# A local-attention stage on one Trainium2 core: its period in a new order, with the scores in two halves

## The chip, the core and the metric

The program runs on one core of a Trainium2 chip. Its engines work side by side, each through its own queue of instructions in order: TensorE (PE; its weight loads are shown apart, as PEld), VectorE (DVE), ScalarE (ACT), GpSimd (POOL), and SyncE (SP), which here issues DMAs. They wait for each other by semaphores. The products go to PSUM, which this kernel divides into eight banks, each a tile of 128 x 512 fp32; VectorE and ScalarE read them there.

The metric is the device time of one execution in microseconds (us): the median of three runs. The trace comes from one more execution, under the profiler.

## What is computed

The reference is a chain of eight blocks on `x` of shape (4, 512, 128): cross-attentions, two mixtures of experts, a ternary feed-forward. The change touches the sixth, `_L2_ffn`: a local transformer of six layers with 16 heads of 64, windows of 32 tokens that look one window back, keys and queries of unit length with rotary factors, a token shift, and a gated feed-forward of 341 hidden units.

```python
def attn_layer(x, Wqkv, qs, ksc, Wo):
    q, k, v = jnp.split(x @ Wqkv, 3, -1)
    ...
    q = l2norm(q) * qs
    k = l2norm(k) * ksc
    q = q * cos * scale + rotate_half(q) * sin * scale
    k = k * cos * inv + rotate_half(k) * sin * inv
    out = local_attention(q, k, v)
    return out.transpose(0, 2, 1, 3).reshape(b, n, INNER) @ Wo

def local_attention(q, k, v):
    ...
    bk2, bv2 = (look(bk), look(bv))     # this window and the one before it
    sim = jnp.einsum('bhwie,bhwje->bhwij', bq, bk2) * QK_SCALE
    sim = jnp.where(mask, -jnp.finfo(sim.dtype).max, sim)
    attn = jax.nn.softmax(sim, -1)
    return jnp.einsum('bhwij,bhwje->bhwie', attn, bv2).reshape(b, h, n, d)
```

Around it, per layer: `x + attn_layer(shift_tokens(x))`, then the feed-forward with a layer norm, a GELU gate and the two products.

## The kernel before

All of this stage is in `local_transformer` (from L1804). The rows live transposed in `Y[b]`, 128 features x 512 tokens, one for each of the four rows of the batch. A **tile** is 128 tokens of one row in one layer: 6 x 4 x 4 = 96 tiles, in the order of layers, rows, tokens. One **period** of the loop over `n` starts tile `n` and carries on the two before it: `T` is tile `n`, `T1` the one before, `T2` the one before that. A row's feed-forward, `F`, is spread over four periods ("phases"), once all of its tiles have their attention. The order of instructions is written out by hand (`tc.manual_schedule()`): each engine runs its instructions in the order in which the loop issues them, so that order is what the change rewrites. In a period stand, with their engines:

- `queries_or_keys(T, kind, c)` (L1835): one product of 512 columns into a PSUM bank (L1842), and its Square on ScalarE (L1844). Four to a tile: kind 0 queries, 1 keys; c the half of the heads.
- `rotate(T, kind, c)` (L1847): three operations on VectorE, the two rotary products from PSUM (L1852, L1855) and the sum of squares (L1864), then GpSimd's addition (L1865).
- `normalise(T)` (L1868): inverse lengths of all queries and keys, small operations of GpSimd (L1875 to L1881) around ScalarE's Ln and Exp (L1876, L1877), then four scalings on GpSimd (L1884), queries first.
- `turned(T1, kind)` (L1886): eight transposes on TensorE by the helper `to_features` (L617, recorded as L621) and two copies on ScalarE (L1896). For keys GpSimd puts the last window of the tile before in front (L1892, or zeros, L1894).
- `scores(T1)` (L1932): eight small products that write the mask (L1940), then 64 products of 64x32 weights with 64 columns, recorded as 128 (L1949), all into two banks.
- `softmax(T1)` (L1955): on VectorE the largest (L1959) and the subtraction (L1960), on ScalarE Exp (L1965).
- `probabilities(T2)` (L1967): eight transposes of P, two copies on ScalarE (L1970).
- `average(T2, g)` (L1972): 32 small products, recorded as 64, for half of the heads (L1980); `normalised(T2, g)` (L1987) divides on VectorE (L1989, L1990). Both halves use the same two banks in turn.
- `attended(T2)` (L1995): eight transposes of the averages, two copies on ScalarE. `project_out(T2)` (L2001): 16 products of 128 columns (L2004) into the averages' banks; `residual(T2)` (L2007) adds them to `Y` on VectorE (L2011).
- `values(T, x0)` (L1905): a product of 512 columns (L1919), ScalarE's copy (L1920), and DMAs on SP's queue (L1922 to L1930) that shift values by a window; they are read two periods later.
- the feed-forward in `ff_stage` (L2074): in phase 0 transposes and moments, later `ff_norm`, four scalings on VectorE (L559); in phase 1 transposes back and two gate products; in phase 2 the third gate product and two up products; in phase 3 the third and the down product. They use the scores' banks.

PSUM: two banks for the products, two for transposes and values (`p_tr`), two for scores and feed-forward (`pair("sc")`), two for averages and projection (`pair("av")`). A piece that takes a bank waits until its last reader is done.

On TensorE a period runs: queries 0, P's transposes, queries 1, the feed-forward's first piece, average 0, queries turned, keys product 0, average 1, keys turned, keys product 1, averages' transposes, all scores, projection, both values, the feed-forward's second piece.

Of the kernel before, what the change touches and what calls it, by code (L numbers as in the profile page):

```python
# [21 lines left out]
F32 = mybir.dt.float32  # L22
# [4 lines left out]
ALU = mybir.AluOpType  # L27
# [3 lines left out]
NT = S // 128  # L31
# [241 lines left out]
def tile_kernel(ctx: ExitStack, tc: tile.TileContext, A: dict, out: bass.AP):  # L273
# [1530 lines left out]
    def local_transformer(Y, lf, lw, columns, tabs):  # L1804

        with ExitStack() as es:
# [21 lines left out]
            class Tile:  # L1828


                def __init__(self, i, b, tt):
                    self.i, self.b, self.tt = i, b, tt
                    self.rot, self.raw, self.ss = {}, {}, None

# [32 lines left out]

            def normalise(T):  # L1868


                n = 2 * LH
                ss = T.ss.rearrange("p a b -> p (a b)")
                y = small.tile([128, n], F32, name="rn_y")
                t = small.tile([128, n], F32, name="rn_t")
                G.tensor_scalar(ss, ss, 1e-24, -0.5, ALU.max, ALU.mult)  # L1875
                SC.activation(y, ss, AF.Ln, scale=-2.0)  # L1876
                SC.activation(y, y, AF.Exp, scale=-0.5)  # L1877
                G.tensor_tensor(t, y, y, ALU.mult)
                G.tensor_tensor(t, t, ss, ALU.mult)
                G.tensor_scalar(t, t, 1.5, None, ALU.add)  # L1880
                G.tensor_tensor(y, y, t, ALU.mult)  # L1881
                for (kind, c), a in sorted(T.rot.items()):
                    o = LH * kind + 8 * c
                    G.tensor_tensor(a, a, bc(y[:, o : o + 8], [128, 8, LD], 2), ALU.mult)  # L1884

            def turned(T, kind):  # L1886


                lead = 32 * kind
                t = qp.tile([128, LH // 2, lead + 128], F32, name="kT" if kind else "qT")  # L1890
                if kind and T.tt:
                    G.tensor_copy(t[:, :, 0:32], T.before.kT[:, :, 128:160])  # L1892
                elif kind:
                    G.memset(t[:, :, 0:32], 0.0)  # L1894
                for c in range(2):
# [3 lines left out]
                    )  # L1899
                if kind:  # L1900
                    T.kT = t
                else:
                    T.qT = t

# [26 lines left out]

            def scores(T):  # L1932

                T.banks = pair("sc").rearrange("p z (k d) -> p z k d", d=64)
                for w in range(4):
                    for z in range(2):
                        r = slice(64 * (z ^ (w // 2)), 64 * (z ^ (w // 2)) + 64)
                        PE.matmul(  # L1940
                            T.banks[32 * w : 32 * w + 32, z], identb[r, r.start : r.start + 32],
                            maskw[r, int(w + T.tt == 0)], start=True, stop=False,
                            skip_group_check=True,
                        )
                for k in range(LH // 2):
                    for w in range(4):
# [7 lines left out]

            def softmax(T):  # L1955

                P = tp.tile([128, LH // 2, 2, LD], F32, name="P", bufs=1)
                mx = small.tile([128, 2, LH // 2], F32, name="la_mx")
                V.tensor_reduce(mx, T.banks, AX.X, ALU.max)  # L1959
                V.tensor_tensor(  # L1960
                    P.rearrange("p k z d -> p z k d"), T.banks,
                    bc(mx, [128, 2, LH // 2, LD], 3), ALU.subtract,
                )
                T.P = P.rearrange("p k z d -> p k (z d)")
                SC.activation(T.P, T.P, AF.Exp, scale=8.0)  # L1965
# [55 lines left out]

            def ff_norm(F):
                layernorm(F.xn, F.xn, F.found)

# [48 lines left out]

            def ff_stage(F, phase, second):  # L2074
                F.w1, F.w2 = loaded[F.i][2:]
                if phase == 0 and not second:
                    ff_moments(F)
                elif phase == 1:
                    ff_gate(F, 0, 1) if second else ff_turn(F)
                elif phase == 2 and second:  # L2080
                    ff_up(F, 0, 1)
                elif phase == 2:
                    ff_gate(F, 2)
                    SC.preload_act_table_set(EXP_LN)
                elif phase == 3:
                    ff_down(F) if second else ff_up(F, 2)

            tiles = [Tile(i, b, tt) for i in range(DEPTH) for b in range(B) for tt in range(NT)]  # L2090
# [3 lines left out]
            SC.preload_act_table_set(EXP_LN)  # L2094
            for n in range(len(tiles) + 2):
                T = tiles[n] if n < len(tiles) else None
                T1 = tiles[n - 1] if 0 <= n - 1 < len(tiles) else None
                T2 = tiles[n - 2] if 0 <= n - 2 < len(tiles) else None
                m, phase = divmod(n - 6, 4)
                F = rows[m] if 0 <= m < len(rows) else None  # L2100
                if T:
# [12 lines left out]
                    T.tabs = tabs[T.i]  # L2114
                    queries_or_keys(T, 0, 0)
                if T2:
                    probabilities(T2)
                if T:
                    queries_or_keys(T, 0, 1)
                    rotate(T, 0, 0)  # L2120
                if F:
                    ff_stage(F, phase, False)
                if T2:
                    average(T2, 0)
                if T1:
                    turned(T1, 0)
                if T:
                    queries_or_keys(T, 1, 0)
                if T2:
                    normalised(T2, 0)  # L2130
                if T:
                    rotate(T, 0, 1)
                if T2:
                    average(T2, 1)
                if T1:
                    turned(T1, 1)
                if T:
                    queries_or_keys(T, 1, 1)
                if T2:
                    normalised(T2, 1)  # L2140
                if T:
                    rotate(T, 1, 0)
                if T2:
                    attended(T2)
                if T and T.tt == NT - 1 and n + 1 < len(tiles):
                    swap(tiles[n + 1].b)
                if T1:
                    scores(T1)
                if T:
                    rotate(T, 1, 1)  # L2150
                if T:
                    normalise(T)
                if T1:
                    softmax(T1)
                if T2:
                    project_out(T2)
                    residual(T2)
                if F and phase == 0:
                    ff_norm(F)
                if T:  # L2160
                    values(T, 0)
                    values(T, 1)
                if F:
                    ff_stage(F, phase, True)
            return loaded[DEPTH - 1][2:]
# [133 lines left out]
```

## Time and profile before

| | us |
|---|---|
| median of three runs (2460.44 to 2462.8) | 2462.42 |
| the profiled execution, its own time | 2456.04 |
| its span, first to last instruction | 2454.2 |
| first query product of the local stage starts | 516.4 |
| first query product of its last tile starts | 2125.35 |
| mean distance of such products, tiles 10 to 90 | 17.01 |
| mean granted clock of TensorE over the span | 0.953 |

The 96 tiles of the local stage take two thirds of the span. In the profile's rows, "PE" with a line number is a matmul group of TensorE, "x2" or "x128" the instructions merged in it; each fp32 product is recorded as two matmuls with a weight load each. In brackets stands the idle time of the engine just before, and what ended it; "issue" means that nothing which the profile shows ended it. A line with a window in front gives busy us and instruction counts of PE, PEld, DVE, ACT and POOL in that window, then granted clock, DMA share and GB/s. Queue q8 is one of the two that carry instructions.

### The profile page before, as it was taken

Reading aid. Unit: us, or ns where it says so; the run is one execution under the profiler, and the core shown is the slowest. Engines: PE = TensorE matmul, PEld = TensorE weight load, DVE = VectorE, ACT = ScalarE, POOL = GpSimd, SP = SyncE. Lnnn points to the kernel's source line nnn. Section 1 sums busy time; section 2 is a strip of 40 time slices with the busy share of each in tenths; the row PEclk is TensorE's granted clock in tenths of the full one; section 3 lists DMA queues with packets and bytes.
Section 4 is the critical chain, followed back from the end, with each engine's and each line's share of the span. In section 5 each row is a group of like instructions: output and inputs, shape, how many; then the busy total and the mean of one; then the engine's idle time right before and its main releaser. Section 6 shows DMA issues by size and latency. Waiting matters only on the chain. (4 is left out here: it accounts for less than half of the span.)

```text
span 2454.2 us, 86703 instructions
## 1 busy us (share of the span) xinstructions
PE 2228.0 (91%) x37341; PEld 1479.5 (60%) x37341; DVE 1759.3 (72%) x3896; ACT 1298.1 (53%) x2389; POOL 1338.6 (55%) x1862
## 2 busy tenths in 40 slices
PE   7958969978999999999999999999999999989676
PEld 3536734546666666666666666666666666644355
DVE  5545356866888888777887888887878788767422
ACT  3423325645666655666666666565666666525222
POOL 2141330256667676766667766766667666710433
PEclk9868989988999999999999999999999999989688
DMA  7201110016211121111211121111211111120023
GB/s 182 68 21 41 40 60 2 1 41 135 80 35 29 35 70 36 33 29 35 75 31 36 29 79 33 29 35 27 80 31 31 35 29 35 27 67 23 26 67 95
DMA packets 134298, 116.14 MB, mean 47 GB/s; under 512 B 29506, under 2 KB 102701, under 8 KB 133917
## 3 DMA queue, kind: packets, MB, share of 16 engines
q1 hardware_dynamic: 122037, 99.67, 15.8%
q0 software_dynamic: 4608, 7.35, 0.9%
q8 instruction: 296, 4.85, 0.9%
q10 hardware_dynamic: 7271, 3.58, 0.5%
q14 instruction: 86, 0.70, 0.1%
HBM read 42.84 MB, written 21.52 MB: 26 GB/s over the span
## 5 line engine op out<-in xcount | busy, mean ns | idle before, releaser
L1865 POOL TENSOR_TENSOR rc<-rc,rs 128x512 f32<-128x512 f32 x384 | 489.8, 1276 | 400.7 <-DVE rs L1855 326.3
L1842 PE MATMUL ps_mm<-wqk,y 128*128 128x512 f32 x768 | 397.2, 599 | 5.3 <-issue 3.5
L1884 POOL TENSOR_TENSOR rc<-rc,rn_y 128x512 f32<-128x512 f32 x384 | 388.6, 1044 | 7.5
L1852 DVE TENSOR_TENSOR rc<-ps_mm,tabs 128x512 f32<-128x512 f32 x384 | 262.5, 684 | 129.8 <-ACT sq L1844 126.5
L1844 ACT ACTIVATE sq<-ps_mm 128x512 f32<-128x512 f32 x384 | 231.2, 602 | 161.4 <-PE ps_mm L1842 108.0
L1855 DVE TENSOR_TENSOR rs<-ps_mm,tabs 128x512 f32<-128x512 f32 x384 | 261.5, 681 | 0.2 <-POOL rc L1865 0.2
L1864 DVE TENSOR_REDUCE ss<-sq 128x8 f32<-128x512 f32 x384 | 259.5, 676 | 0.0
L621 PE MATMUL ps_tr<-cst,rc 128*128 128x128 f32 x1536 | 210.9, 280 | 4.3 <-POOL rc L1884 4.0
L1980 PEld LDWEIGHTS ps_av<-v,PT 64*32 64x32 f32 x12288 | 138.1, 105 | 126.5 <-PE ps_tr L621 54.1
L2004 PE MATMUL ps_av<-aT,wo 128*128 128x128 f32 x1536 | 200.7, 283 | 2.4 <-issue 2.4
L2004 PEld LDWEIGHTS ps_av<-aT,wo 128*128 128x128 f32 x1536 | 181.0, 193 | 12.6 <-issue 3.9
L621 PEld LDWEIGHTS ps_tr<-cst,rc 128*128 128x128 f32 x1536 | 165.6, 142 | 24.4 <-POOL rc L1884 5.1
L1949 PE MATMUL ps_sc<-kT,qT 64*32 64x64 f32 x12288 | 148.1, 225 | 33.6 <-issue 32.9
L1980 PE MATMUL ps_av<-v,PT 64*32 64x65 f32 x12288 | 170.3, 225 | 6.2 <-DVE attn L1990 1.7
L1949 PEld LDWEIGHTS ps_sc<-kT,qT 64*32 64x32 f32 x12288 | 141.2, 105 | 44.2 <-issue 38.1
L1056 POOL DMA_INDIRECT back<-ye,to x80 | 78.8, 985 | 147.5 <-DVE ye L1170 104.0
L1842 PEld LDWEIGHTS ps_mm<-wqk,y 128*128 128x128 f32 x768 | 124.5, 192 | 56.3 <-issue 50.1
L1965 ACT ACTIVATE P<-P 128x1024 f32<-128x1024 f32 x96 | 101.4, 1057 | 97.3 <-DVE P L1960 97.3
L1876 ACT ACTIVATE rn_y<-ss 128x32 f32<-128x32 f32 x96 | 22.0, 229 | 237.9 <-POOL ss L1875 237.9
L802 ACT ACTIVATE P<-ps,deltaT 77x512 f32<-77x512 f32 x192 | 115.8, 683 | 56.7 <-PE ps L796 53.0
L1896 ACT COPY qT<-ps_tr 128x512 f32<-128x512 f32 x192 | 103.3, 589 | 74.6 <-PE ps_tr L621 74.3
L1959 DVE TENSOR_REDUCE la_mx<-ps_sc 128x16 f32<-128x1024 f32 x96 | 116.9, 1218 | 31.0 <-PE ps_sc L1949 31.0
(399 smaller groups left out, 4368.9 us busy)
## 6 DMA issues: line engine op xcount, KB each, us to landing
v<-v SPq DMA_DIRECT2D x432, 65.0 KB
v<-v SPq DMA_DIRECT2D x96, 195.0 KB
wqk<-in_L_ffn_Wqkv_dram SPq DMA_DIRECT2D x24, 256.0 KB
sent<-xn SPq DMA_DIRECT2D x2, 2210.0 KB
xe<-sent SPq DMA_DIRECT2D x16, 260.0 KB
back<-xn SPq DMA_DIRECT2D x2, 2048.0 KB
raw<-in_L_ffn_W_dram SPq DMA_DIRECT2D x8, 512.0 KB
w<-in_L_ffn_W_dram SPq DMA_DIRECT2D x16, 256.0 KB
```

Source lines behind the costliest of these rows:

```text
L621: PE.transpose(t[:, i], src[:, i], ident)
L1842: PE.matmul(t, lhs, T.w[2 * kind + c], start=True, stop=True)
L1844: SC.activation(sq, t, AF.Square)
L1852: V.tensor_tensor(a, t, bc(T.tabs[:, 2 * kind, tt], [128, 8, LD], 1), ALU.mult)
L1855: V.tensor_tensor(r.rearrange("p h (x d) -> p h x d", x=2), t.rearrange("p h (x d) -> p h x d", x=2)[:, :, ::-1], bc(T.tabs[:, 2 * kind + ...
L1864: V.tensor_reduce(T.ss[:, kind, 8 * c : 8 * c + 8], sq, AX.X, ALU.add)
L1865: G.tensor_tensor(a, a, r, ALU.add)
L1884: G.tensor_tensor(a, a, bc(y[:, o : o + 8], [128, 8, LD], 2), ALU.mult)
L1949: PE.matmul(T.banks[32 * w : 32 * w + 32, z, k], T.qT[r, k, 32 * w : 32 * w + 32], T.kT[r, k, 32 * w : 32 * w + 64], start=False, stop=Tru ...
L1959: V.tensor_reduce(mx, T.banks, AX.X, ALU.max)
L1980: PE.matmul(T.means[32 * w : 32 * w + 32, x0, k], T.PT[r, 4 * g + k, 32 * w : 32 * w + 32], (T.v1 if w % 2 else T.v2)[r, x0, 4 * g + k], s ...
L2004: PE.matmul(t, T.wo[:, c], T.aT[:, c], start=(c == 0), stop=(c == 7))
```

## The change

The period becomes a table of stages, each with its lag in tiles, and the loop walks through it. Some functions are cut in two so that the table can place their parts: `normalise` into `inverse_norms` and `normalise(T, kind)`, `softmax` into `largest` and `exponentials`, `scores` into two halves of four of its eight column groups, the keys' first window of `turned` into `keys_before`, `ff_stage` into `ff_first` and `ff_second`. The computation stays the same, and so do all buffers.

On TensorE a period now runs: values 0, keys product 0, P's transposes, the feed-forward's second piece (one period later than before), average 0, queries product 1, keys turned, the feed-forward's first piece, queries turned, average 1, keys product 1, mask and scores' first half, queries product 0, averages' transposes, scores' second half, values 1, projection. `residual` stands at the head of the next period, `ff_norm` behind it. VectorE's rotation of queries product 0 stands in front of `largest`. The loop has one period more.

```diff
+            def inverse_norms(T):
...
+                T.inv = y
+
+            def normalise(T, kind):
+                for c in range(2):
+                    a, o = T.rot[kind, c], LH * kind + 8 * c
+                    G.tensor_tensor(a, a, bc(T.inv[:, o : o + 8], [128, 8, LD], 2), ALU.mult)
...
+            def keys_before(T):
+
+                T.kT = qp.tile([128, LH // 2, 160], F32, name="kT")
+                if T.tt:
+                    G.tensor_copy(T.kT[:, :, 0:32], T.before.kT[:, :, 128:160])
                 else:
+                    G.memset(T.kT[:, :, 0:32], 0.0)
...
-            def scores(T):
...
+            def scores(T, g):
+                if g == 0:
+                    T.banks = pair("sc").rearrange("p z (k d) -> p z k d", d=64)
...
-                for k in range(LH // 2):
+                for k in range(4 * g, 4 * g + 4):
...
+            def largest(T):
+                T.mx = small.tile([128, 2, LH // 2], F32, name="la_mx")
+                V.tensor_reduce(T.mx, T.banks, AX.X, ALU.max)
+
+            def exponentials(T):
                 P = tp.tile([128, LH // 2, 2, LD], F32, name="P", bufs=1)
...
+            period = (
+                (values, 0, 0),
+                (residual, 3),
+                (ff_norm, 1),
+                (queries_or_keys, 0, 1, 0),
+                (rotate, 0, 1, 0),
+                (keys_before, 1),
+                (probabilities, 2),
+                (ff_second, 1),
+                (average, 2, 0),
+                (queries_or_keys, 0, 0, 1),
+                (turned, 1, 1),
+                (normalised, 2, 0),
+                (rotate, 0, 0, 1),
+                (ff_first, 0),
+                (turned, 1, 0),
+                (average, 2, 1),
+                (queries_or_keys, 0, 1, 1),
+                (normalised, 2, 1),
+                (scores, 1, 0),
+                (queries_or_keys, 0, 0, 0),
+                (attended, 2),
+                (rotate, 0, 1, 1),
+                (scores, 1, 1),
+                (rotate, 0, 0, 0),
+                (values, 0, 1),
+                (largest, 1),
+                (inverse_norms, 0),
+                (normalise, 0, 0),
+                (project_out, 2),
+                (normalise, 0, 1),
+                (exponentials, 1),
+            )
...
-            for n in range(len(tiles) + 2):
+            for n in range(len(tiles) + 3):
...
+                for stage, lag, *which in period:
+                    if stage in by_row:
+                        m, phase = divmod(n - lag - 6, 4)
+                        if 0 <= m < len(rows) - 1:
+                            F = rows[m]
+                            F.w1, F.w2 = loaded[F.i][2:]
+                            stage(F, phase)
+                    elif 0 <= n - lag < len(tiles):
+                        stage(tiles[n - lag], *which)
```

## The prediction

> **What bounds the kernel now.** I read the page first, for the engines' shares and the queues, then the engines' busy time by stretches of 100 us, then TensorE's timeline over some periods, then the waits.
>
> ```profile
> PE 2228.0 (91%) x37341; PEld 1479.5 (60%) x37341; DVE 1759.3 (72%) x3896; ACT 1298.1 (53%) x2389; POOL 1338.6 (55%) x1862
> q8 instruction: 296, 4.85, 0.9%
> ```
>
> ```profile
> 900.00:1000.00 100.00, 99.17 (x1985) 67.18 (x1984) 82.19 (x142) 66.43 (x120) 69.55 (x98) 1.00 0.22 60
> 1000.00:1100.00 100.00, 96.39 (x1970) 65.42 (x1968) 81.45 (x147) 57.47 (x106) 70.08 (x99) 1.00 0.12 32
> ```
>
> In the local stage (516 to 2170 us) TensorE is the engine without air: 96 to 99% busy at a granted clock of 1.00, VectorE next with 82. So the period is the sum of TensorE's pieces plus its waits, and I look for the waits in its timeline:
>
> ```profile
> 1005.61 1.02 PE L1842 MATMUL ps_mm<-wqk,y 128*128 128x512 f32 x2
> 1006.56 0.86 PE L1980 MATMUL ps_av<-v,PT 64*32 64x65 f32 x64
> 1007.36 1.09 PE L621 MATMUL ps_tr<-cst,rc 128*128 128x128 f32 x8
> 1008.28 1.02 PE L1842 MATMUL ps_mm<-wqk,y 128*128 128x512 f32 x2
> 1009.14 1.04 PE L621 MATMUL ps_tr<-cst,attn 128*128 128x128 f32 x8
> 1010.11 0.41 PE L1940 MATMUL ps_sc<-maskw,identb 64*32 64x512 bf16 x8
> 1010.34 1.41 PE L1949 MATMUL ps_sc<-kT,qT 64*32 64x64 f32 x123
> 1012.80 0.31 PE L1949 MATMUL ps_sc<-kT,qT 64*32 64x64 f32 x5 [1.06 <-issue]
> 1013.04 2.05 PE L2004 MATMUL ps_av<-aT,wo 128*128 128x128 f32 x16
> ...
> 1029.00 1.46 PE L1949 MATMUL ps_sc<-kT,qT 64*32 64x64 f32 x128
> 1030.39 2.05 PE L2004 MATMUL ps_av<-aT,wo 128*128 128x128 f32 x16
> ```
>
> Start to start is a piece's price: 128 scores take 1.39 us (1029.00 to 1030.39), but 2.70 from 1010.34. Nothing of the program ends that wait ("issue"). It is the **instruction fetch**: queue q8 moved 4.85 MB in 296 packets, 16.4 KB each, and TensorE's 2 x 37341 instructions, with 1107 semaphore instructions in its records, make that 64 B an instruction, 256 a packet. Counted off, the score waits stand at the same place modulo 256. Where the queue had already run dry one packet earlier, the next comes 5.0 to 5.3 us after it (634.28 to 639.55, 771.15 to 776.18, 823.39 to 828.59, 1041.48 to 1046.79). I use 5.1 us a packet.
>
> Between 600 and 2100 us, 88 periods of 17.0 us, I took each piece's start to start less its quickest. The excess is 68.5 us, 0.78 a period: scores 39.4, projection 5.5 and about 7 in the averages are fetch, 0.59 a period; the rest, 0.19, is waiting for other engines (P's transposes 0.07, the averages behind the moments 0.05, the feed-forward's turn 0.04). At most 0.78 x 95 = 74 us can be won.
>
> **Part 1, the fetch waits: -0.42 us a period.** From the first average to the last score the old order issues 128+16+4+128+16+4+16+272 = 584 instructions in 0.78+0.93+0.95+0.78+0.93+0.86+0.97+0.23+1.39 = 7.8 us; at 5.1 us a packet they ask 11.6. Read-ahead covers 3.8 less 0.59, 3.2 us. The new order has some 596 there, over 0.78+0.94+0.87+0.65+0.97+0.78+1.03+0.23+0.78+0.94+0.97+0.78 = 9.7 us (0.65 is the mean of the feed-forward's first pieces, 0.44, 0.44, 0.86 and 0.86; products, entrances and halves are priced in part 2); they ask 11.9. The shortfall is 2.2: below the cover, so none on average (bound: 0), or in proportion 0.59 x 2.2/3.8 = 0.34 (bound), as a packet's border may fall badly. I take the middle, 0.17.
>
> [...]
>
> **Part 2, the split on TensorE: +0.36.** A product in front of transposes takes 0.86 (1008.28 to 1009.14), in front of small tiles 0.95: entering costs 0.09, and there is one more entrance. Sixty-four pairs of the averages take 0.78, 128 scores 1.39, so two halves are 2 x 0.78 - 1.39 = 0.17 dearer: a group pays for its ramp and for 0.147 from its last start to the next piece. Leaving: the first transpose behind the averages lasts 329 ns instead of 272, the first projection matmul 377 instead of 275; four leavings in front of products at about 0.08 against 0.06+0.06+0.10 before, +0.10. Bounds: 0.15 if the drains overlap with what follows, 0.45 with 0.10 for each leaving. I take the sum, since the averages are the same form of work.
>
> **Part 3, the softmax chain in front of P's transposes: +0.12.** The rows:
>
> ```profile
> 2123.82 1.22 DVE L1960 TENSOR_TENSOR P<-ps_sc,la_mx 128x1024 f32<-128x1024 f32 x1
> 2125.07 1.06 ACT L1965 ACTIVATE P<-P 128x1024 f32<-128x1024 f32 x1 [0.66 <-DVE P L1960]
> 2125.55 3.45 DVE L559 TENSOR_SCALAR xn<-xn,ln_mv,ln_rs 128x128 f32<-128x128 f32 x4
> 2126.04 1.06 ACT L1920 COPY v<-ps_tr 128x512 f32<-128x512 f32 x2
> 2126.66 1.15 PE L621 MATMUL ps_tr<-cst,P 128*128 128x128 f32 x8 [0.29 <-ACT v L1920]
> ```
>
> VectorE's rotation of the last query product now stands ahead of `largest`. From that product's start: 1.06 to its Square, 0.63 to the rotation, 1.79 for its three operations, 1.25 maximum, 1.25 subtraction, 1.10 Exp, together 7.08 until P can be turned. TensorE gets there after 0.94 product, 0.97 attn's transposes, 0.78 half, 0.94 values, 1.78 projection, 0.86 values, 0.86 keys, 7.13. No slack; and P's second four need the bank that the values copy frees 0.53 after Exp, against 0.44 for the first four: 0.09. With phases in which VectorE comes later I take 0.19, less the 0.07 of before. If part 2 comes cheap, this grows by 0.1. Behind the wait stand the feed-forward's second half and both averages.
>
> **Part 4, ScalarE's queue and the moved pieces: +0.08-0.12 = -0.04.** ScalarE has the values copy and a Square ahead of P's copies; in the one period of four without a second feed-forward piece the first average waits about 0.4 for them: +0.08 with small change. Gone are the averages' wait behind the moments (0.05) and the turn's for the scalings (0.04, and some 0.03 inside its quickest). At nothing: the scalings (3.45 us, 1.0 each beside GpSimd's normalising) move to the period's head, hidden by eight of TensorE's pieces; the keys' rotation and the first `normalised` stand behind them and end just as the second average needs the bank. GpSimd normalises the keys last though they are turned first. From the last query product's start: 3.0 to its add, 1.35 for that, 0.94+0.32+0.34+0.39+0.33 for the norms, 1.0 for each of four scalings, so 9.7 and 10.7 for the two key tiles; without a second feed-forward piece TensorE wants them at 7.2+0.96+0.4+0.87+0.94 = 10.4 and 10.8, otherwise 0.9 to 2.6 later. The values' DMAs on SP's queue, half now issued at the head, are read two periods later. The residual holds the projection's bank until the first average, 2.5 us on.
>
> **Start and end: +5 us.** Each tile begins with values, and the first needs `wv`, whose packets run from 516.1 to 518.6 us where the first product started at 516.36: 1 to 3 us. The keys, normalised last (2 x 1.0 us) and turned first, add 2. The extra period holds a residual and a down product, which were at the end before. Bounds 2 to 9.
>
> **The sum.** -0.42+0.36+0.12-0.04 = +0.02 a period, x 95 = +2; with the start +7. The profiled execution took 2456.04 us (span 2454.2), 6.4 below the runs' median of 2462.42; 2463.0 beside it is **2469.4** beside the median.
>
> [...]
>
> **Rivals.** (a) Faster: the waits go entirely and the second half's drain is hidden. -0.59+0.19+0.18 (parts 3 and 4 with the 0.1) = -0.22 x 95 + 5 = -16, **2446**. For it: the shortfall is below the cover. Against: averages, the same form, pay in full. It decides where a half takes under 0.70. (b) The chain of part 3 becomes the bound: 0.6 a period before P instead of 0.19, +0.4 x 95, **2507**. For: no slack in 7.08 against 7.13. Against: its pieces vary by hundredths. (c) The split doesn't do what it says: borders fall into the second half as before and 0.45 of fetch wait stays: +0.28 x 95, **2496**. For: the instructions are nearly the same number.
>
> **Numbers.** Forecast 0.51, (a) 0.25, (b) 0.12, (c) 0.12. The forecast's own range is 2455 to 2484. Extremes: all low, -0.59+0.15+0.22-0.04 = -0.26 a period and 2 at the start, 2440; all high, -0.25+0.45+0.22 = +0.42 and 9, 2511. For 8 in 10 I cut to 2446 to 2497, which leaves out half of (b) and the ends. No change means within 0.2%, 2457.5 to 2467.3. Faster: (a) and 0.03 of the forecast, 0.28; same 0.18, slower 0.54.
>
> **What would show it.** Scores' excess from 39.4 us down to 10 to 18 in as many periods (part 1); each half 0.77 to 0.80 to the next piece (part 2); idle before P's transposes of 0.1 to 0.25 in most periods (part 3). Wrong if halves take 0.70, if P's wait passes 0.4, or if the score waits stay.

## The result, and the profile after

| | before | after |
|---|---|---|
| median of four runs, us | 2462.61 (2460.44 to 2466.53) | 2492.41 (2483.09 to 2493.77) |
| the profiled execution, its span | 2456.04, 2454.2 | 2483.09, 2481.2 |
| mean distance of query products, tiles 10 to 90 | 17.01 | 17.20 |
| from the last piece before the stage to tile 10's first query or key product | 166.6 | 177.9 |

The ratio of the runs is 1.011, with a 95% interval of 1.0093 to 1.0127: slower by 1.1%, 29.8 us by the medians, where +7 was forecast. In the profiled executions the last tile starts 28.8 us later, counted from the piece in front of the stage: 11.25 up to tile 10, 17.5 in the 85 periods behind it. The rest of the program gives 2 us back.

On the page of the kernel after, TensorE is busy for 53 us more with the same 37341 matmuls, and the instruction queue moves almost the same bytes:

```profile
PE 2281.0 (92%) x37341; PEld 1484.6 (60%) x37341; DVE 1773.2 (71%) x3896; ACT 1291.3 (52%) x2389; POOL 1336.9 (54%) x1862
q8 instruction: 295, 4.83, 0.8%
```

In two stretches of 100 us (columns as before) it is 99% busy at full clock in both; before it was 99 and 96:

```profile
900.00:1000.00 100.00, 99.14 (x1974) 66.36 (x1974) 84.25 (x148) 58.95 (x110) 67.25 (x92) 1.00 0.22 58
1000.00:1100.00 100.00, 99.25 (x1901) 64.49 (x1900) 78.69 (x136) 61.20 (x111) 68.84 (x100) 1.00 0.12 32
```

So most of the waits have gone, and the kernel is slower: the pieces have grown. TensorE's waits from 600 to 2100 us, by what ended them (us in total, times, longest; waits under 0.15 us are not in this list), first before:

```profile
PE ps_sc L1949 <- issue: 31.6, 30, 2.2
PE ps_sc L2028 <- DVE xn L559: 3.0, 8, 0.5
```

and after:

```profile
PE ps_av L1986 <- ACT PT L1976: 7.5, 24, 0.3
PE ps_sc L1954 <- issue: 4.8, 6, 2.3
PE ps_sc L1954 <- POOL kT L1905: 2.1, 5, 0.5
```

The scores' fetch wait falls from 31.6 to 4.8 us, the turn's wait for VectorE's scalings is gone, and two new ones have come. TensorE's timeline of the kernel after, from the scores' first half to the projection:

```profile
1011.89 0.84 PE L1954 MATMUL ps_sc<-kT,qT 64*32 64x64 f32 x64
1012.66 1.12 PE L1842 MATMUL ps_mm<-wqk,y 128*128 128x512 f32 x2
1013.62 1.04 PE L621 MATMUL ps_tr<-cst,attn 128*128 128x128 f32 x8
1014.59 0.99 PE L1954 MATMUL ps_sc<-kT,qT 64*32 64x64 f32 x64
1015.51 1.12 PE L1923 MATMUL ps_tr<-wv,yw 128*128 128x512 f32 x2
1016.47 1.95 PE L2010 MATMUL ps_av<-aT,wo 128*128 128x128 f32 x16
```

Start to start, the first half takes 0.77 (1011.89 to 1012.66), and a product behind small tiles 0.96 (1012.66 to 1013.62; 1015.51 to 1016.47), where one behind large tiles takes 0.86. The second half has a short fetch wait here (0.92 instead of 0.79). A period without a second feed-forward piece:

```profile
1055.16 1.13 PE L621 MATMUL ps_tr<-cst,P 128*128 128x128 f32 x8
1056.61 1.00 PE L1986 MATMUL ps_av<-v,PT 64*32 64x65 f32 x64 [0.32 <-ACT PT L1976]
1057.54 1.12 PE L1842 MATMUL ps_mm<-wqk,y 128*128 128x512 f32 x2
...
1062.76 0.41 PE L1944 MATMUL ps_sc<-maskw,identb 64*32 64x512 bf16 x8
1063.60 0.86 PE L1954 MATMUL ps_sc<-kT,qT 64*32 64x64 f32 x64 [0.44 <-POOL kT L1905]
```

From P's transposes to the average it takes 1.45 instead of 0.97, the average itself 0.93 instead of 0.79, and the scores wait for GpSimd's copy of the last window. Two rows of GpSimd show what stood in front of that copy:

```profile
1058.85 0.74 POOL L1792 TENSOR_TENSOR tabs<-cst,qs 128x256 f32<-128x256 f32 x1
...
1063.15 0.40 POOL L1905 COPY kT<-kT 128x256 f32<-128x256 f32 x1
```

From 1058.85 to 1061.86 GpSimd prepares the rotary tables of the next layer (L1792, L1798), which it does once in 16 periods. All five waits of the list above stand behind such tables (788.6, 1063.6, 1338.3, 1615.2 and 1889.6 us); in the other periods the copy is in time.

### The profile page after: what moved, and what is told of

It is laid out like the page before. It is cut to its first block, busy times and chain, and to the rows that moved or that the text cites. A ratio compares the mean times of both kernels' runs of the same rounds, so it can differ in the third digit from the quotient of the medians.

```text
span 2481.2 us, 86349 instructions
## 1 busy us (share of the span) xinstructions
PE 2281.0 (92%) x37341; PEld 1484.6 (60%) x37341; DVE 1773.2 (71%) x3896; ACT 1291.3 (52%) x2389; POOL 1336.9 (54%) x1862
## 3 DMA queue, kind: packets, MB, share of 16 engines
q1 hardware_dynamic: 122037, 99.67, 15.9%
## 4 chain that ended last, share of the span: by engine, by line
PE 72%; issue 9%; DVE 7%; POOL 4%; ACT 4%; DMA 4%; SPq 1%; POOLq 0%; another core or an unknown queue 0%; DVEq 0%; ACTq 0%
PE ps_mm L1842 13%; PE ps_tr L621 12%; PE ps_tr L1923 6%; PE ps_av L1986 6%; PE ps_sc L1954 5%; PE ps_av L2010 5%; PE ps_sc L2057 2%; PE ps_sc L2069 2%; PE ps_sc L2046 2%; DMA v<-v 1%; PE ps L812 1%; PE ps L1354 1%; PE ps L1717 1%; PE ps L821 1%; PE ps L796 1%
## 5 line engine op out<-in xcount | busy, mean ns | idle before, releaser
L1842 PE MATMUL ps_mm<-wqk,y 128*128 128x512 f32 x768 | 425.4, 636 | 0.8 <-DVE rs L1855 0.8
L621 PEld LDWEIGHTS ps_tr<-cst,rc 128*128 128x128 f32 x1536 | 176.0, 142 | 93.6 <-issue 49.0
L2010 PEld LDWEIGHTS ps_av<-aT,wo 128*128 128x128 f32 x1536 | 188.1, 193 | 45.3 <-issue 45.3
L2010 PE MATMUL ps_av<-aT,wo 128*128 128x128 f32 x1536 | 188.7, 276 | 0.0
L1954 PE MATMUL ps_sc<-kT,qT 64*32 64x64 f32 x12288 | 166.0, 224 | 8.0 <-issue 4.8
L1924 ACT COPY v<-ps_tr 128x512 f32<-128x512 f32 x192 | 111.0, 578 | 104.1 <-PE ps_tr L1923 104.1
L1996 DVE TENSOR_TENSOR attn<-ps_av,la_den 128x512 f32<-128x512 f32 x192 | 132.8, 692 | 6.6
L621 PEld LDWEIGHTS ps_tr<-cst,P 128*128 128x128 f32 x768 | 81.1, 141 | 80.9 <-ACT P L1971 74.3
```

The costliest lines, as they stand in the source:

```text
L621: PE.transpose(t[:, i], src[:, i], ident)
L1842: PE.matmul(t, lhs, T.w[2 * kind + c], start=True, stop=True)
L1954: PE.matmul(T.banks[32 * w : 32 * w + 32, z, k], T.qT[r, k, 32 * w : 32 * w + 32], T.kT[r, k, 32 * w : 32 * w + 64], start=False, stop=Tru ...
L2010: PE.matmul(t, T.wo[:, c], T.aT[:, c], start=(c == 0), stop=(c == 7))
```

## The experiments

Each kernel was run beside the kernel before on the same chip. The chips differ by 2% (medians of the kernel before from 2406.42 to 2461.16 us), so ratios to before are compared, and the traces' mean distance of tiles 10 to 90.

| kernel | ratio to before, 95% interval | period, us |
|---|---|---|
| after | 1.0110 (1.0093 to 1.0127) | 17.20 |
| only_averages_between | 1.0050 (1.0024 to 1.0076) | 17.01 |
| undivided | 1.0112 (1.0086 to 1.0139) | 17.15 |
| query_before_average | 1.0077 (1.0053 to 1.0102) | 17.15 |
| keys_first | 1.0145 (1.0118 to 1.0172) | 17.29 |
| combined | 1.0021 (1.0006 to 1.0036) | 16.98 |
| split_alone | 1.0110 (1.0084 to 1.0135) | 17.23 |
| turn_later | 1.0322 (1.0297 to 1.0348) | 17.89 |
| split_covered | 1.0321 (1.0292 to 1.0349) | 17.91 |
| spread | 0.9948 (0.9925 to 0.9971) | 16.85 |
| spread_more | 0.9845 (0.9820 to 0.9870) | 16.69 |
| spread_more_split | 1.0046 (1.0031 to 1.0061) | 17.15 |

**1. The queries' product out of the split (only_averages_between).**

```diff
+                (queries_or_keys, 0, 0, 0),
                 (scores, 1, 0),
-                (queries_or_keys, 0, 0, 0),
                 (attended, 2),
```

> The changed kernel with queries product 0 moved in front of the mask, so that only the averages' transposes stand between the two halves of the scores. My theory: one leaving goes in front of transposes (0.06) instead of a product (0.10), -0.04 us a period; the softmax chain, which starts at that product, gets some 1.0 us of TensorE's work more ahead of P's transposes, so their wait of 0.07 and the 0.095 behind the second four vanish, -0.14. Together -0.18 x 95 = -17: 2475 us; the halves stand 0.96 closer, so up to 0.1 a period of fetch wait may return: 2475 to 2484. Rival (the softmax chain costs nothing, since the next wait takes its place): -4, 2488.

Measured: median 2469.52, ratio 1.0050, a period 0.19 shorter than after's, beside the theory's 0.18. TensorE's timeline shows the pieces:

```profile
1053.30 0.84 PE L1954 MATMUL ps_sc<-kT,qT 64*32 64x64 f32 x64
1054.07 1.09 PE L621 MATMUL ps_tr<-cst,attn 128*128 128x128 f32 x8
1055.09 0.86 PE L1954 MATMUL ps_sc<-kT,qT 64*32 64x64 f32 x64
```

The transposes behind the first half take 1.02 (1054.07 to 1055.09) where they took 0.97 behind a product (1013.62 to 1014.59 above): leaving costs 0.056 in front of transposes and 0.10 in front of a product. The mean wait before P's transposes falls from 0.07 to 0.03 a period, and goes almost altogether in three of the four phases. The softmax chain's price was real, but 0.09 a period instead of 0.14; the leaving gives 0.05, and another 0.05 are waits at the mask, for GpSimd's window and one fetch wait, which the theory did not name. That the sum is the theory's is in part luck.

**2. The split taken out of that order (undivided).**

```diff
+                (attended, 2),
                 (scores, 1, 0),
-                (attended, 2),
-                (rotate, 0, 1, 1),
                 (scores, 1, 1),
+                (rotate, 0, 1, 1),
```

> As the kernel with only the averages' transposes between the halves, but those transposes go in front too: all scores in one group again, in the new order. The two kernels differ in the split alone. My theory (the split is paid on TensorE and repaid by the fetch): TensorE's pieces 0.23 a period cheaper (ramp 0.17, the mode change 0.06), -22 us; the scores' fetch waits come back, 0.3 to 0.4 a period, +28 to +38; so 5 to 15 us slower than the kernel with the averages between, 2480 to 2495, with 25 to 40 us of excess in the scores over 88 periods. Rival (the spread order, not the split, took the fetch waits away): 22 us faster than that kernel, near 2453, and the scores' excess stays below 12 us.

Measured: 16.6 us slower than the kernel above by the medians, a little more than the theory's 5 to 15. On TensorE the pieces are 0.32 a period cheaper (5.363 against 5.685 from the products in front of the mask to the second values product), more than the 0.23 I had written, because the entrance (0.094) counts too; the 0.06 beside the ramp is the leaving in front of transposes, 0.056 in experiment 1. The scores' excess is 22.3 us against 6.4, less than the 25 to 40 expected. So another wait is in the difference: P's transposes wait 0.24 a period against 0.03. The scores are not the reason: they end 0.32 us earlier behind average 1 than in the kernel above (5.19 against 5.51, medians of some 87 periods). But VectorE's `largest` starts 6.29 us behind average 1 in both kernels, since VectorE is busy with the rotations until then; it sat idle for the undivided scores in only 6 periods of 87. So P is ready no sooner, and TensorE waits for it through a large part of what it saves.

So the rival fell by its own mark (12 us), but not wholly: the new order without the split has 22.3 us of excess in the scores where the old one had 39.4. Of the split's own sum, 0.32 a period is paid and 0.21 repaid (15.9 us in the scores, 3.0 in the projection's neighbour, over 88 periods); the 0.20 of P's wait makes undivided the slower one.

**3. A product between P's transposes and the average (query_before_average).**

```diff
+                (queries_or_keys, 0, 0, 1),
                 (average, 2, 0),
-                (queries_or_keys, 0, 0, 1),
                 (turned, 1, 1),
```

> The changed kernel with queries product 1 moved in front of average 0, so a product stands between P's transposes and the average where there is no feed-forward piece. My theory: in those periods (22 of 88, and some 9 at the start, where the feed-forward hasn't begun) the average waits 0.48 for ScalarE's copies and takes 0.14 longer; 0.62 x 31 = -19; the leaving stands in front of transposes, -0.04 x 95 = -4. But the turned keys then come 0.86 earlier behind the average, and GpSimd's scalings may give back 0.3 to 0.6 in those periods. 2470 to 2482. Rival (GpSimd's chain of the keys is what really ends those periods): only the -4, 2488.

Measured: median 2477.28, inside the expectation; the ratio says 1.0077, 8 us less than after's, and the trace has its last tile 8.4 earlier, 3.7 of it up to tile 10. The average no longer waits for ScalarE in the period without a feed-forward piece, but the keys' transposes behind it now wait for GpSimd's scalings:

```profile
1051.20 0.86 PE L1986 MATMUL ps_av<-v,PT 64*32 64x65 f32 x64
1052.05 0.66 PE L621 MATMUL ps_tr<-cst,rc 128*128 128x128 f32 x4
1053.05 0.66 PE L621 MATMUL ps_tr<-cst,rc 128*128 128x128 f32 x4 [0.34 <-POOL rc L1887]
```

From the keys' transposes to the turn of the feed-forward it takes 1.49 in these periods instead of 0.93: 0.56 of the 0.62 won come back there.

**4. The keys' scalings ahead of the queries' (keys_first).**

```diff
+                (normalise, 0, 1),
                 (normalise, 0, 0),
                 (project_out, 2),
-                (normalise, 0, 1),
```

> The changed kernel with the keys' two scalings on GpSimd in front of the queries' two. My theory: the scores' wait for GpSimd's copy of the first window (0.14 and 0.07 in two of four periods) and the turned tiles' small waits shrink, -0.05 x 95, and 2 us at the start: 2485. Rival (GpSimd's order makes no difference in the steady state, the queries being then late instead): 2489 to 2494.

Measured: median 2493.04, inside the rival's span; by the ratio, 1.0145 against 1.0110 with overlapping intervals, it is rather slower than after, and in the trace its last tile starts 2.9 us later. Tile 10 starts 4.4 us earlier than in after, twice the 2 expected, but the periods are 0.09 longer: now the queries come late, and the piece of the feed-forward in front of their transposes takes 0.545 instead of 0.44 to 0.455 in two of four phases, which is 0.05 of the 0.09. The five waits for GpSimd's window stay (1.8 us), as the tables stand behind the scalings of both kinds.

**5. Both moves together (combined).** It holds the diffs of 1, 3 and 4.

> The changed kernel with both moves that helped (queries product 0 in front of the mask, queries product 1 in front of average 0), and the keys scaled first. My theory: the two gains, 23 and 15 us, are different waits and add up: 2492 - 38 = 2454, 2448 to 2462, level with the kernel before or a little faster. Rival (GpSimd's chain of the keys, which the earlier turned keys now wait for, eats the second gain): 2465 to 2470.

Measured: ratio 1.0021, which is 2466 beside the 2461 of before that the expectation was made from: the rival's time. But not GpSimd is waited for; the first row of TensorE's waits is the second average's for VectorE's division:

```profile
PE ps_av L1986 <- DVE attn L1996: 7.8, 22, 0.4
```

The two gains in ratio, 0.0060 and 0.0033, would make 1.0017, inside the interval, and were smaller than the 38 us that the medians of 1 and 3 seemed to give. With the 0.0035 that the keys' scalings lost in experiment 4 the sum would be 1.0052: that loss seems not to have come along, though the single ratios are no better known than by some 0.0025.

**6. The split alone in the old order (split_alone).**

```diff
-                    scores(T1)
+                    scores(T1, 0)
+                if T:
+                    values(T, 0)
+                if T1:
+                    scores(T1, 1)
...
-                    values(T, 0)
                     values(T, 1)
```

> The kernel before, in its old order, with the scores in two halves and the first values product between them; nothing else moved. My theory (the split is paid on TensorE and repaid by the fetch): one more entrance 0.094, a second ramp 0.173 and a leaving in front of a product 0.10 make +0.37 a period, x 95 = +35; of the fetch waits, 52 us in 88 periods, 35 to 43 go: 8 us faster to 5 us slower than before, 2453 to 2466, with 10 us or less of excess in the scores. Rival (the old order is too dense for the split to help): two thirds of the fetch waits stay, +20, 2481.

Measured: ratio 1.0110, 24 us slower by the medians, past the rival's 20; but not for the rival's reason. The split's own sum came out: the pieces are 0.366 a period dearer (0.772 + 1.056 + 0.788 against 1.389 + 0.861), and the scores' excess falls from 39.4 us in 88 periods to 8.0 in 85, 0.35 a period. What was not in the sum stands behind it in the timeline:

```profile
1023.37 0.83 PE L2029 MATMUL ps_sc<-cst,xn 128*128 128x128 f32 x3
1024.87 0.33 PE L2029 MATMUL ps_sc<-cst,xn 128*128 128x128 f32 x1 [0.67 <-DVE xn L559]
```

The feed-forward's turn waits for VectorE's last scaling: 1.68 on average from its start to the average where it took 0.92. The values product that now stands between the halves was the cover behind the projection. In one period of four that makes 0.19 a period, x 95 = 18 us. The rest is in the feed-forward's second pieces, which take 0.065 longer each than before (2.643 against 2.578, 1.782 against 1.717), 5 us. The trace shows why: they take the scores' banks, and start 0.156 us (median) behind the end of VectorE's subtraction, the last reader of these banks, where it was 0.9 before; their first matmul lasts 657 ns instead of 592. The same values product was the cover here too.

**7. The control and the split under cover (turn_later, split_covered).** Both put the feed-forward's first piece behind `normalised(T2, 0)`, in front of average 1; the first in the kernel before, the second in the split-alone kernel.

```diff
-                if F:
-                    ff_stage(F, phase, False)
                 if T2:
                     average(T2, 0)
...
                     normalised(T2, 0)
+                if F:
+                    ff_stage(F, phase, False)
```

> The kernel before, in its old order, with the feed-forward's first piece moved from in front of average 0 to in front of average 1; the control for the next kernel. My theory: it takes away the averages' wait behind the moments (0.05 a period) and the turn's small waits (0.04), and moves nothing else: 0 to 9 us faster, ratio 0.996 to 1.000.

> The split-alone kernel (the old order, a values product between the halves) with the same move of the feed-forward's first piece. In the split-alone kernel the split itself balanced, +0.366 a period on TensorE against -0.36 of fetch, and the 24 us it lost are the turn's wait for VectorE's scalings, 0.95 in one period of four, because the values product no longer stands in front of it. My theory: with 1.7 to 2.6 us more ahead of the turn that wait goes, and the kernel is within 5 us of the control, ratio to before 0.995 to 1.002. Rival (the split itself costs the 24 us; the wait at the turn only shows where they end): 20 to 27 us slower than the control, ratio 1.007 to 1.011.

Measured: 1.0322 and 1.0321. The control's expectation was far off: 78 us slower, not 0 to 9 faster. The moments and products of the feed-forward now stand on VectorE ahead of the rotation of queries product 1, whose bank keys product 1 needs. It is the first line of the control's waits on TensorE over the whole run, and nearly all of it (35.1 us) is keys product 1:

```profile
PE ps_mm L1842 <- DVE rs L1855: 36.5, 50, 1.3
```

The pair differs in the split alone, though, and is equal to 0.0001: the theory's statement, but on a base that has other waits for a difference to hide in. That it is neutral there, with 0.366 a period of price and 24 us less excess in the scores (33.9 to 10.1), also rests on smaller waits in the other pieces.

**8. Another order, undivided (spread).** The table in full; the two halves of the scores follow each other on TensorE, as nothing between them is work of TensorE:

```python
(queries_or_keys, 0, 1, 0), (inverse_norms, 1), (normalise, 1, 1), (exponentials, 2),
(values, 1, 1), (project_out, 3), (normalise, 1, 0), (rotate, 0, 1, 0), (keys_before, 1),
(probabilities, 2), (residual, 3), (ff_second, 1), (queries_or_keys, 0, 0, 1),
(average, 2, 0), (turned, 1, 1), (ff_norm, 1), (normalised, 2, 0), (rotate, 0, 0, 1),
(ff_first, 0), (queries_or_keys, 0, 1, 1), (turned, 1, 0), (average, 2, 1),
(queries_or_keys, 0, 0, 0), (values, 0, 0), (scores, 1, 0), (rotate, 0, 1, 1),
(normalised, 2, 1), (rotate, 0, 0, 0), (scores, 1, 1), (attended, 2), (largest, 1),
```

> Another order from the same table: scores undivided, with two products (queries 0 and values 0) between average 1 and the scores, the averages' transposes behind the scores, queries 1 in front of average 0, and the second values product and ScalarE's Exp each moved across the period's border. My theory: three groups of small tiles instead of four save 0.32 a period against the kernel with the averages between, 30 us; of the fetch waits some 20 us stay more than there, since 272 instructions stand together; P's chain has 2.7 us more: 2430 to 2455, faster than both. Rival (undivided scores bring back the fetch and the wait before P as they did in the undivided kernel): 2470 to 2490.

Measured: ratio 0.9948, faster than undivided and only_averages_between, and within the theory's span. The undivided scores have 2.1 us of excess in 86 periods, where some 20 more than there had been allowed: the rival fell. The kernel differs from undivided by several moves at once, and no run takes them apart. In the list of TensorE's waits from 600 to 2060 us "issue" doesn't occur any more; it begins:

```profile
PE ps_sc L2035 <- DVE xn L559: 17.1, 32, 0.9
PE ps_tr L621 <- ACT P L1971: 13.3, 23, 1.9
```

These two are the longest of what is left: the turn waits for VectorE's scalings, and P's transposes wait for Exp. Of their 13.3 us, 9.7 are five waits of 1.9 us, one in 16 periods: GpSimd's tables of the next layer (1006.01 to 1009.09 us) stand in front of the inverse norms, whose Ln and Exp stand in front of P's Exp in ScalarE's queue. The other 18 waits are 0.2 each.

**9. The same, with the feed-forward's first piece later (spread_more).** Again in full:

```python
(normalise, 1, 0), (largest, 2), (queries_or_keys, 0, 1, 0), (exponentials, 2),
(normalise, 1, 1), (rotate, 0, 1, 0), (queries_or_keys, 0, 0, 1), (keys_before, 1),
(project_out, 3), (residual, 3), (probabilities, 2), (ff_second, 1), (average, 2, 0),
(turned, 1, 0), (queries_or_keys, 0, 1, 1), (ff_norm, 1), (turned, 1, 1),
(normalised, 2, 0), (rotate, 0, 0, 1), (rotate, 0, 1, 1), (ff_first, 0), (average, 2, 1),
(values, 0, 0), (normalised, 2, 1), (queries_or_keys, 0, 0, 0), (values, 0, 1),
(scores, 1, 0), (scores, 1, 1), (rotate, 0, 0, 0), (attended, 2), (inverse_norms, 0),
```

> The spread order once more, with the feed-forward's first piece behind keys product 1 and both turns (in the spread kernel its turn waited 24 us in 22 periods for VectorE's scalings, and P's transposes 17), and three products (values 0, queries 0, values 1) between average 1 and the undivided scores. My theory: the turn's wait goes, 20 us, and P's stays or shrinks: ratio 0.984 to 0.992. Rival (VectorE's work in the period with the moments is the bound, and the wait moves to P): 0.993 to 0.998.

Measured: 2384.54 beside 2420.79, ratio 0.9845 (0.9820 to 0.9870): the best kernel of this study, 1.55% below before and 2.6% below after. As the theory said, neither the turn's wait for the scalings nor P's for Exp is among its waits from 600 to 2060 us any more; the first in the list, 7.4 us, is that of the keys' and queries' transposes for GpSimd's scalings. Against spread, the traces' last tile starts 13 us earlier, where the ratios, from two chips, differ by 25. In its timeline average 1, three products (one shown) and the scores stand without a wait:

```profile
1002.60 0.86 PE L1986 MATMUL ps_av<-v,PT 64*32 64x65 f32 x64
1003.39 1.12 PE L1923 MATMUL ps_tr<-wv,y 128*128 128x512 f32 x2
...
1006.39 1.46 PE L1954 MATMUL ps_sc<-kT,qT 64*32 64x64 f32 x128
1007.78 1.09 PE L621 MATMUL ps_tr<-cst,attn 128*128 128x128 f32 x8
```

**10. The split in that order (spread_more_split).**

```diff
                 (scores, 1, 0),
+                (attended, 2),
                 (scores, 1, 1),
                 (rotate, 0, 0, 0),
-                (attended, 2),
```

> The spread-more order with the scores in two halves around the averages' transposes, which stand behind the undivided scores there; nothing else moved. In that order the undivided scores have 4.2 us of fetch wait in 88 periods, so there is little left to repay a split. My theory: the split costs what it cost on TensorE before, 0.32 a period (entrance 0.094, ramp 0.173, leaving 0.056), x 95 = +30, less 4 of fetch: 26 us slower than the spread-more kernel, ratio to before 0.994 to 0.997. Rival (the fetch wait is a matter of the scores' own 272 instructions, and most of it hides inside other waits): the split still gains, ratio 0.980 to 0.985.

Measured: ratio 1.0046, 0.020 above spread_more, 49 us where 26 were expected; the rival fell. The pieces are 0.364 a period dearer (4.628 against 4.264 from the mask to the projection; the second half now leaves in front of a product, which I had priced as before transposes), and P's transposes wait 0.17 more, since the scores end a piece later: here VectorE's `largest` does wait for them, in all 85 periods, 79 us in total. The scores' excess falls by 2.8 us in all. Here is the same split with nothing to repay it.

## Why the prediction was right and wrong

The direction was the one held likelier, and the time lies in the range of 2446 to 2497, but above the forecast's own 2455 to 2484: +7 became +30. The excesses below are those of the prediction, taken the same way.

| step | forecast, us a period | measured |
|---|---|---|
| part 1, fetch | -0.42 | -0.45 |
| part 2, split on TensorE | +0.36 | +0.455 |
| part 3, softmax chain | +0.12 | +0.06 |
| part 4, ScalarE's queue and the moved pieces | -0.04 | +0.115 |
| sum | +0.02 | +0.18 (the trace: +0.185) |
| start | +5 us | +11.25 us up to tile 10 |

**Part 1 was right.** The scores' excess is 3.3 us in the first halves and 4.2 in the second, from 39.4 (10 to 18 forecast); with the waits at the mask, the averages and the projection some 12.5 us in 88 periods, 0.14 where 0.17 was written. That these waits are the instruction fetch holds in the other traces too: counted in TensorE's records, semaphore instructions among them, 66 of the 67 "issue" waits over 0.15 us from 600 to 2100 us in before, after and undivided stand at 193 to 195 modulo 256, and in before and after 47 of 48 end 1.2 to 1.7 us behind the end of a packet of q8 (the one at 1012.80 behind the packet from 1010.35 to 1011.32). The read-ahead is in the trace of before too: from 600 to 2100 us TensorE comes to that place in its count 1.2 to 8.5 us behind the packet's end, 3.5 in the median. The 3.2 us of cover was an estimate with 5.1 us a packet, and 5.1 is no limit: in before the starts of two packets are 3.4 us apart at the closest (1044.43 and 1047.86 among others). Rival (c), 0.45 of fetch wait left, fell, though its 2496 lies nearest to the time. That a stretch asks more packets than it has time for, at 5.1 us each, fits this change (3.8 us more before, 2.2 after), but it doesn't order all kernels: by the same count, from average 0 to the last score, undivided (592 instructions in 9.4 us) asks 2.35 us more than its stretch lasts and spread (576 in 8.5) 3.0, and their scores' excesses are 22.3 and 2.1. What besides the shortfall decides, where the borders fall or what stands just before the scores, stays open; it wasn't tried.

**Part 2 had one term too small.** The halves came as priced (0.772 and 0.788; their ramp 0.17), the entrance too (0.094). The step "four leavings in front of products at about 0.08" is the one that failed: each is 0.102, four make 0.41, less 0.22 before, +0.19 instead of +0.10; the sum is then the 0.45 that had been written as the upper bound. The two rows from which 0.08 was taken, 329 against 272 ns and 377 against 275, were two different prices, one for transposes and one for full products, and the second was the right one. Rival (a), which hid what the second half pays from its last start to the next piece, fell: no half takes under 0.70, and that stretch is 0.146 behind either half.

**Part 3 was too dear.** The wait before P's transposes is 0.07 a period and the second four add 0.07, together 0.14 instead of 0.19; rival (b), 0.6, fell. Experiment 1 gave the chain more cover and won 0.09 of it back.

**Part 4 is the largest miss, 0.155 a period.** What I took off went (the averages behind the moments, the turn). The wait of the average for ScalarE's copies was forecast at 0.4 in one period of four and is 0.48. But "+0.08 with small change" left out what stands behind it: the average that comes out of that wait takes 0.14 longer, the second average waits 0.11 and 0.07 in two phases, for which I had written that the keys' rotation and the first `normalised` "end just as the second average needs the bank", and the scores wait 0.14 in one phase for GpSimd's first window, which I had not priced at all. As an average 0.14 hides what it is: five waits, one in 16 periods, behind the next layer's tables. Together these make 0.235 instead of 0.08. Things costed at nothing had too little slack in one phase each. Experiment 3 confirms the place of the first, and shows that behind it GpSimd's keys were nearly as late.

**The start was mis-sized, by 4 to 6.** Ten periods at 0.18 are 1.8 of the 11.25. The two terms written for it came: the first product waits for `wv`, as said, and comes 2.4 us later with respect to the stage before (1 to 3 forecast), and the keys, normalised last and turned first, add 2:

```profile
519.86 2.05 PE L1923 MATMUL ps_tr<-wv,y 128*128 128x512 f32 x2 [3.78 <-DMA wv<-in_L_ffn_Wqkv_dram]
537.80 3.91 PE L621 MATMUL ps_tr<-cst,rc 128*128 128x128 f32 x16 [5.70 <-POOL rc L1887]
```

The keys of tile 0 keep TensorE waiting for 5.7 us where it was 3.69 before, for the queries. What the sum left out comes behind: the first transposes of P are 7.0 us later than before, and until the feed-forward begins every period is one without a second piece, so each pays the 0.48 and its followers. I had priced that wait for one period of four only. Experiments 3 and 4 bring tile 10 forward by 3.7 and 4.4 us.

**The split as such.** Four pairs differ in it alone (TensorE's price a period; the scores' excess; the ratio's change): the old order, 0.366, 39.4 to 8.0 us, +0.011; the new order around the averages, 0.32, 22.3 to 6.4, -0.006; the control pair, 0.366, 33.9 to 10.1, 0.000; spread_more, 0.364, 4.2 to 1.4, +0.020. It never won more from the fetch than it cost, and where it was ahead it was because TensorE would otherwise have waited for P. The change paid for the fetch with entrances and leavings; two other orders, spread and spread_more, are as free of these waits with undivided scores. Which of their moves did that is not shown: they have two and three products between average 1 and the scores, but undivided has two products and the averages' transposes there, and 22.3 us of excess. TensorE's rows show 0.094 for entering, 0.056 or 0.10 for leaving.

## What to carry to other kernels

On an engine that is 97% busy (TensorE before, 600 to 2100 us), an order that removes waits by cutting groups in two must be costed with every entrance and leaving (here 0.094, and 0.056 or 0.10 us), each by the row with the same next piece. A piece moved to break up one stretch was somebody's cover: name what stood behind it in every phase, the pipeline's filling included, and whatever is hidden "just in time" should be given a price. List waits one by one before averaging them by phase: what comes once a layer looks like small change in every period. Before cutting a dense group, try other orders of whole pieces; two of the three tried here with undivided scores left them almost without fetch waits (2.1 and 4.2 us of excess, 39.4 before).

## What the runs showed of the hardware that was not expected

- Leaving a group of 64x32 tiles has two prices here: 0.056 us when transposes follow (before: eight transposes take 0.929 behind an average, 0.873 behind a product), 0.10 when a full product follows (after: 0.962 behind small tiles, 0.860 behind large ones).
- In the kernel after, an average that starts right after its wait for ScalarE's copies takes 0.93 us (median of 24; 1056.61 to 1057.54) instead of 0.79 with the same 64 matmuls. Nothing in the trace stands in its way; what makes it longer is not shown.
- The scores' excess can stand or go with the same matmuls in another order: 39.4 us before and 7.5 after, with 37341 matmuls on both pages, and 2.1 in spread, which is made of the same stages as after.
